# A table in DRAM of the token in each expert slot, biases gathered per slot, a reordered opening, and seven-product multiplications in the first pass

## The chip, the cores and the metric

The kernel runs on one core of one Trainium2 chip. Its time is the device time of one execution in microseconds; of several runs the median is given. The core's engines are TensorE (PE, with its weight loads as PEld), VectorE (DVE), ScalarE (ACT), GpSimd (POOL) and SyncE (SP), which here issues most of the plain DMAs. Everything is computed in fp32.

## The reference

Two layers work on 2048 tokens of width 512 (8 sequences of 256). In the first layer all of this is computed from the normalized tokens:

```python
xn = layernorm(x)
# attention of 32 heads of 128, with decay over the distance of two tokens
q, k, v = silu(xn @ qkv_w.T)            # 3 * 32 * 128 columns
attn = decayed_linear_attention(q, k, v)
attn = rms_normalized(attn) * norm_w
x1 = x + (sigmoid(xn @ gate_w.T) * attn) @ out_w.T
# mixture of experts: 16 experts of inner width 128, two for each token
scores = softmax(xn @ router_w + router_b) + router_bias
gate[t, e] = scores[t, e] for the two best experts of the two best groups, else 0
y = sum_e gate[:, e] * ((silu(xn @ ew1[e] + eb1[e]) * (xn @ ew2[e] + eb2[e])) @ ew3[e] + eb3[e])
# a shared expert, of inner width 256, for every token
z = (silu(xn @ sw1 + sb1) * (xn @ sw2 + sb2)) @ sw3 + sb3
x = x1 + y + z
```

The second layer normalizes again and adds a single-head attention of width 128 and a gated sum of 64 low-rank maps of rank 16, of which each token uses the 16 with the highest scores (`Wr`).

## The kernel before

Tokens are worked on in four chunks of 512 (`NCH`; index `i`), each of four row tiles of 128 (`TPC`; index `t`).

**The opening** (`work1` pool, L140 to L525) goes over the chunks. It loads x (L150, L169), normalizes it (`normalize`, L226), turns it (`turn_rows`, L240, PE transposes into `xT`), multiplies it by the shared expert's first weights (`shared_up`, L317), scores the experts (`route`, L265; `first_two` at L250 compares all pairs of values), and in `shared_down` (L329) multiplies by the shared expert's second weights. There the gates, with a column of ones for the shared expert, are turned (L333), copied (L335) and multiplied by the 17 rows of `b3` (L338): this puts the gated biases of all experts and the shared bias into the same bank as the product (L340), and the bank is added to x (L341), which L349 stores in `xr`. `token_sums` (L369) forms sums of token blocks on POOL, `decays` (L357) the attention's decay tables on ACT, stored in `dec`, and `clear` (L410) fills a quarter of `xd` with zeros: `xd` has 512 columns for each of 6016 expert slots (47 tiles of 128, each tile with a single expert). Then the dispatch (L446 to L523) works out on DVE which slot each token has (`slots`), what its gate is (`slot_gates`) and which weight rows each tile needs (`rows_`). The tiles of the dispatch and its inputs lie in part in the opening's pool, whose memory the next pool, `attn`, takes over.

**The first layer's passes** (L1177 on): chunk `i` against eight groups `g` of four heads. One pair `(i, g)` is a unit, multiplying a 512 x 512 token block by 512 x 2048 weights. The multiplication is done by Strassen's scheme on two levels: on the outer one each unit has seven products (`Outer`, in `ORDER`), on the inner one each of these has seven again (`p1` to `p7`, L1037 to L1066), or eight where it is `plain` (L981). One inner product is four matmuls of 128 x 128 x 128 (`product`, L661, recorded as L666, with two instructions for each). Before, all outers of the first pass (`i == 0`) are plain, and those of the later passes are sevenfold. A sevenfold outer's last product, `p3`, is run inside the next outer.

The weights of an outer are prepared in the first pass (`weights`, L605): a 1 MB block is loaded, outer sums are formed on DVE from further blocks (`st`), four inner sums on POOL (L635), and the result is stored in `ws` for the later passes. Three outers, those in `RAW` (p1, p2, p4), need no outer sums. These steps are popped one by one while the outer before it runs (`following.step()`, L991). `prepare(n + 2)` makes the outer after next; weights are held in a ring of three buffers, blocks `st` and the experts' data in two (`staged`).

PE and DVE are ordered by the scheduler; ACT and POOL keep the program's order in this part (`manual_schedule`, L599). Everything that is not an outer product is a piece put in by `later(n, f)`: it runs `n` products from now. For each quarter of a unit (half of the batch rows, two heads) the pieces are Silu and gate on ACT, scores, attention and output projection on PE. In the first pass, two pieces a unit (`row`, L1086) load a row tile of normalized tokens and scatter it twice into `xd` (L1094). From the second pass on two or three experts per unit are worked in (`expert`, L1080): SP loads 128 rows from `xd` (L696), POOL gathers weights (L697), PE turns the rows 8 products later (L706), multiplies 11 later (L716) and 14 later (L728), ACT copies the result, SP stores it in `yd`. At a chunk's end `load_sum` (L933) loads `xr`, and `finish` (L586) adds the attention. `wrapped_up` (L1145) gathers chunk 0's expert rows, adds them with their gates (`settle`) and normalizes the sum.

**The second layer** (L1258 on) does the same four chunks one after another. `Head` (L1302) holds its router (`route`, 64 columns), `qk`, `values` and `softmax`; for chunk 0 they are run one after another (L1396), for the others as fillers between products.

## Time and profile before

| | |
|---|---|
| median of three runs (lowest, highest) | 2854.79 us (2854.20, 2859.41) |
| the profiled execution | 2856.16 us, span 2854.4 us |
| mean granted clock of TensorE | 0.993 |
| busy share of the span | PE 98%, DVE 55%, ACT 33%, POOL 51% |
| moved by DMA | 763.21 MB, mean 267 GB/s |

The profile is of one execution. An engine's busy time is that of its instructions; issuing DMAs and waiting for semaphores does not count. Matmuls overlap in the pipeline, so the mean duration of one (276 ns for L666) is longer than the step from one to the next, and a PE that is called busy can still run at a low clock; the granted clock is 1.0 at full speed. "x" before a number is a count of instructions, of which an fp32 matmul has two. Where a line shows a number in brackets with an arrow, the engine stood idle so long before, and what follows the arrow is what it waited for. L97 is the helper through which all elementwise tensor operations go, so these are told apart by their tiles.

### The profile page before, as it was taken

How to read it: one execution, taken by the hardware profiler on the slowest of the kernel's cores; microseconds unless marked ns; L12 is line 12 of the kernel's file. 1: busy time of each engine (PE TensorE's matmuls, PEld its weight loads, DVE VectorE, ACT ScalarE, POOL GpSimd, SP SyncE). 2: the span in 40 equal slices, each digit the busy share in tenths (PEclk: the TensorE clock that was granted, in tenths of full speed). 3: DMA queues.
4: the chain of work that ended last, by engine and by line, in shares of the span. 5: the costliest groups of instructions: out<-in, count | busy, mean ns of one | idle time of the engine just before them, and what ended most of it. 6: DMA issues, size and time to landing. Idle time of an engine off the chain costs nothing. (4 is left out here: it accounts for less than half of the span.)

```text
span 2854.4 us, 49572 instructions
## 1 busy us (share of the span) xinstructions
PE 2796.7 (98%) x19864; PEld 2566.1 (90%) x19864; DVE 1569.7 (55%) x2615; ACT 948.2 (33%) x1683; POOL 1465.7 (51%) x1213
## 2 busy tenths in 40 slices
PE   8989999999999999999999999999999999999999
PEld 4469999999999999999999999999999999987877
DVE  6555666666654445444545555555555555556663
ACT  3312222212244333333443333443444333432221
POOL 4545666665546555555645454545544566552210
PEclk9999999999999999999999999999999999999999
DMA  7888998899986777778877777777777788652211
GB/s 255 301 309 337 357 352 341 341 349 347 364 320 246 262 266 273 282 270 299 296 265 257 264 266 265 259 274 280 284 259 259 267 310 298 222 212 88 76 61 61
DMA packets 161943, 763.21 MB, mean 267 GB/s; under 512 B 18209, under 2 KB 24225, under 8 KB 109874
## 3 DMA queue, kind: packets, MB, share of 16 engines
q1 hardware_dynamic: 149826, 706.25, 66.9%
q0 software_dynamic: 11888, 53.79, 5.2%
q8 instruction: 157, 2.57, 0.4%
q14 instruction: 72, 0.59, 0.1%
HBM read 596.14 MB, written 163.05 MB: 266 GB/s over the span
## 5 line engine op out<-in xcount | busy, mean ns | idle before, releaser
L666 PE MATMUL ps_a<-xt,w 128*128 128x128 f32 x5376 | 750.9, 276 | 11.7 <-DVE r L97 7.7
L666 PEld LDWEIGHTS ps_a<-xt,w 128*128 128x128 f32 x5376 | 681.9, 192 | 30.1 <-issue 14.3
L97 POOL TENSOR_TENSOR c<-c 128x512 f32<-128x512 f32 x216 | 271.7, 1273 | 262.0 <-DVE c L97 259.9
L97 POOL TENSOR_TENSOR c<-c,r 128x512 f32<-128x512 f32 x240 | 318.4, 1347 | 158.9 <-DVE r L97 153.1
L666 PE MATMUL ps_e<-xt,w 128*128 128x128 f32 x2688 | 373.4, 275 | 1.3 <-DVE c L97 1.3
L97 POOL TENSOR_TENSOR sums<-sums,sq 128x512 f32<-128x512 f32 x120 | 153.3, 1278 | 426.4 <-ACT sq L796 425.6
L996 ACT COPY cp<-ps_a 128x512 f32<-128x512 f32 x336 | 196.4, 585 | 476.0 <-PE ps_a L666 468.8
L666 PEld LDWEIGHTS ps_e<-xt,w 128*128 128x128 f32 x2688 | 344.4, 192 | 11.2 <-issue 3.8
L97 POOL TENSOR_TENSOR w<-w 128x512 f32<-128x512 f32 x224 | 294.6, 1325 | 108.2 <-issue 31.2
L666 PE MATMUL ps_a<-w,xt 128*128 128x128 f32 x1792 | 346.7, 275 | 0.0
L858 PE MATMUL ps_sc<-wo,gT 128*128 128x256 f32 x1288 | 305.1, 379 | 1.8 <-POOL gT L97 1.8
L97 DVE TENSOR_TENSOR acc<-ps_sc,acc 128x512 f32<-128x512 f32 x208 | 143.3, 690 | 265.8 <-PE ps_sc L858 198.8
L666 PEld LDWEIGHTS ps_a<-w,xt 128*128 128x128 f32 x1792 | 272.3, 192 | 0.0
L97 DVE TENSOR_TENSOR c<-ps_a,c 128x512 f32<-128x512 f32 x232 | 157.9, 686 | 202.7 <-PE ps_a L666 201.7
L858 PEld LDWEIGHTS ps_sc<-wo,gT 128*128 128x128 f32 x1288 | 232.3, 190 | 26.8 <-POOL gT L97 2.0
L666 PE MATMUL ps_b<-xt,w 128*128 128x128 f32 x1680 | 236.4, 277 | 6.8 <-ACT c L1010 4.2
L801 DVE SCALAR_TENSOR_TENSOR gT<-ps_o,nw,c 128x256 f32<-128x256 f32 x256 | 112.0, 479 | 231.0 <-ACT sq L796 222.0
L666 PEld LDWEIGHTS ps_b<-xt,w 128*128 128x128 f32 x1680 | 217.3, 194 | 17.5 <-issue 8.2
L744 ACT ACTIVATE c<-c 128x512 f32<-128x512 f32 x256 | 148.9, 627 | 170.1 <-DVE c L97 170.0
L796 ACT ACTIVATE sq<-ps_o 128x512 f32<-128x512 f32 x120 | 71.6, 597 | 382.3 <-PE ps_o L782 382.3
L666 PE MATMUL ps_e<-w,xt 128*128 128x128 f32 x896 | 173.2, 275 | 0.0
L97 DVE TENSOR_TENSOR s<-ps_sc,decay 128x384 f32<-128x384 f32 x256 | 139.8, 552 | 40.7 <-PE ps_sc L770 38.1
(299 smaller groups left out, 4635.8 us busy)
## 6 DMA issues: line engine op xcount, KB each, us to landing
w<-in_w_att_dram SPq DMA_DIRECT2D x128, 1024.0 KB
st<-in_w_att_dram SPq DMA_DIRECT2D x32, 1024.0 KB
wo<-in_w_out_dram SPq DMA_DIRECT2D x113, 256.0 KB
decay<-dec SPq DMA_DIRECT2D x64, 384.0 KB
w<-ws0p SPq DMA_DIRECT2D x12, 1792.0 KB
w<-ws1p SPq DMA_DIRECT2D x12, 1792.0 KB
w<-ws2p SPq DMA_DIRECT2D x12, 1792.0 KB
w<-ws3p SPq DMA_DIRECT2D x12, 1792.0 KB
```

The source lines that it names most:

```text
L97: (eng or nc.vector).tensor_tensor(o, a, b, op)
L666: mm(bank[:, bass.ts(ty, P)], a, b, start=(first and ty == 0), stop=True, skip_group_check=True,)
L744: nc.scalar.activation(qk, qk, AF.Silu)
L796: nc.scalar.activation(sq, po, AF.Square)
L801: nc.vector.scalar_tensor_tensor(gT[:, h, :].rearrange("p (t n) -> p t n", t=2), po[:, bass.ts(h, S)].rearrange("p (t n) -> p t n", t=2), ...
L858: mm(py[:, bass.ts(t, S)], self.O[p][:, hh, bass.ts(t, P)], self.wo[p][:, hh, :], start=(t == 0 and hh == 0), stop=(hh == 1), skip_group_c ...
L996: nc.scalar.copy(c, bank)
```

## The change

`xd`, its clears and the row loads go. In their place is `table`: 16 equal int32 values, 64 bytes, for each slot, filled with zero at first; `scatter` writes the tokens' numbers into it, five times in a unit of the first pass, and `read_table` reads it in the pass's last unit and turns it into `whose`, one token number for each slot. An expert gathers its rows from the normalized tokens `xnd` by `whose`, later gathers its output bias into the same place by `own_`, and DVE adds it to the product. The shared bias is added on POOL by `last_bias` when `xr` is loaded.

In the opening, chunk 0 is normalized row tile by row tile, two loads of x and that of `wsh` are issued by ACT, sixteen transposes of the identity run on PE first, the router's matmuls stand between the projections (for the last two chunks also in the scheduled order; for the first two, twelve of the sixteen run ahead of the projections), the next chunk is turned before `shared_down` of the last, the two best experts are found with MAX8 and MATCH_REPLACE8, and what the dispatch reads lies in the `acc` tile.

In the first pass p1, p2 and p4 are sevenfold. Their token sums are formed on POOL once (`first_sums`), their weight sums before the outer begins. All outers of the later passes are sevenfold as before; p6, p5, p3 and p7 of the first pass stay plain. The normalization in `wrapped_up` is cut into pieces, and chunk 0's head in the second layer alternates router and q, k projections.

```diff
+    disp = Parts(accp.tile([P, 7 * CH], FP, tag="acc", name="disp"))
...
-        nc.sync.dma_start(out=xs[0][:, t, :], in_=x_t[0, t])
+        (nc.scalar if t % 2 else nc.sync).dma_start(out=xs[0][:, t, :], in_=x_t[0, t])
...
-    nc.sync.dma_start(out=wsh, in_=w_sh)
...
-    b3_t = held[0 : E + 1, SH * C : (SH + 1) * C]
-    nc.sync.dma_start(out=b3_t, in_=b3)
...
-    xd = dram.tile([NSLOT, C], FP, name="xd")
...
+    table = dram.tile([NSLOT, SAME], I32, name="table")
+    none = once([P, NMT * SAME], "none", I32)
+    nc.vector.memset(none, 0)
+    nc.sync.dma_start(out=table.rearrange("(p j) o -> p (j o)", p=P), in_=none)
...
+    root = small.tile([P, TPC], FP, tag="rstd", name="root")
+    nc.scalar.activation(root[:, 0:1], eps_t, AF.Sqrt)
+    nc.scalar.dma_start(out=wsh, in_=w_sh)
...
+    idle = ps_o()
+    for n in range(WARM):
+        nc.tensor.transpose(idle[:, bass.ts(n % 4, P)], ident, ident)
...
+            n.stats(t, tc.keep_in_program_order if behind and t == 0 else lambda ins: ins)
+            if apart:
+                n.root(t, t + 1)
+                n.scaled(t)
+        if not apart:
+            n.root()
+            for t in range(TPC):
+                n.scaled(t)
...
+    def chosen_two(keep, v):
+        top = scratch[:, 0, 0 : TPC * 8].rearrange("p (t n) -> p t n", t=TPC)
+        rest = scratch[:, 0, TPC * 8 : TPC * (8 + E)].rearrange("p (t n) -> p t n", t=TPC)
+        for t in range(TPC):
+            nc.vector.max(top[:, t, :], v[:, t, :])
+        nc.vector.tensor_copy(pair[:, :, 0:2], top[:, :, 0:2])
+        for t in range(TPC):
+            nc.vector.match_replace(rest[:, t, :], pair[:, t, :], v[:, t, :], -NEVER)
+        nc.vector.tensor_scalar(keep, rest, -NEVER, None, ALU.is_equal)
...
+    def scores(pl, xT, t):
+        for c in range(NC):
+            mm(
+                pl[:, bass.ts(t, E)], xT[:, c, bass.ts(t, P)], rw[:, c, :],
+                start=(c == 0), stop=(c == NC - 1),
+            )
...
-        first_two(sel, masked, E)
-        tt(ge[:, :, 0:E], sc, sel, ALU.mult)
-        nc.vector.memset(ge[:, :, E : E + 1], 1.0)
+        chosen_two(sel, masked)
+        tt(ge, sc, sel, ALU.mult)
...
-    def shared_up(i):
+    def shared_up(i, between):
         hT = scratch[:, 2 + i % 2, :].rearrange("p (e n) -> p e n", e=SH)
         for e in range(SH):
             p1, p2 = ps_mm(), ps_mm()
             project(p1, wsh, e, i)
+            between()
             project(p2, wsh, SH + e, i)
+            between()
             h1 = work.tile([P, CH], FP, tag="h1", name="h1")
             b1, b2 = bsh_t[:, 0, e : e + 1], bsh_t[:, 1, e : e + 1]
...
     def shared_down(i, hT):
         xc = xs[i]
-        pg = ps_sc()
-        for t in range(TPC):
-            nc.tensor.transpose(pg[0 : E + 1, bass.ts(t, P)], gates[i][:, t, :], ident)
-        gT = work.tile([E + 1, CH], FP, tag="geT", name="geT", bufs=1)
-        nc.scalar.copy(gT, pg[0 : E + 1, :])
         for t in range(TPC):
             py = ps_mm()
-            mm(py, gT[:, bass.ts(t, P)], b3_t, start=True, stop=False)
             for e in range(SH):
-                mm(py, hT[:, e, bass.ts(t, P)], w3sh[:, e, :], start=False, stop=(e == SH - 1))
+                mm(py, hT[:, e, bass.ts(t, P)], w3sh[:, e, :], start=(e == 0), stop=(e == SH - 1))
             tt(xc[:, t, :], py, xc[:, t, :], ALU.add)
...
+    sel_all = disp.tile([P, NTT, E], FP, name="sel_all")
...
-    for i in range(NCH):
+    def turn(i):
         xT.append(work.tile([P, NC, CH], FP, tag="xT", name=f"xT{i}", bufs=3))
         for t in range(TPC):
             turn_rows(xT[i], xns[i], t, ps_mm())
-        nc.sync.dma_start(out=xnd[i], in_=xns[i])
+    turn(0)
+    for i in range(NCH):
+        nc.sync.dma_start(
+            out=xnd[i * CH : (i + 1) * CH, :].rearrange("(t p) c -> p t c", p=P), in_=xns[i]
+        )
         if i + 1 < NCH:
             begin(i + 1)
         token_sums(i)
@@ -433,12 +473,14 @@
                 w = big("w")
                 nc.sync.dma_start(out=w[:, 0:4], in_=w_att[0, RAW[p]])
                 first_w.append(w)
-        ups.append(shared_up(i))
-        ge = once([P, TPC, E + 1], f"ge{i}")
-        route(xT[i], ge, sel_all[:, bass.ts(i, TPC), :])
+        pl, tiles = ps_sc(), list(range(TPC))
+        ups.append(shared_up(i, lambda: scores(pl, xT[i], tiles.pop(0))))
+        ge = disp.tile([P, TPC, E], FP, name=f"ge{i}")
+        route(pl, ge, sel_all[:, bass.ts(i, TPC), :])
         gates.append(ge)
+        if i + 1 < NCH:
+            turn(i + 1)
         decays(i)
-        clear(i)
         if i > 0:
             share(i - 1, ups[i - 1])
     share(NCH - 1, ups[-1])
...
+    def last_bias(r, t3):
+        nc.sync.dma_start(out=t3, in_=b3[E : E + 1].to_broadcast([P, C]))
+        for t in range(TPC):
+            add(r[:, t, :], r[:, t, :], t3, nc.gpsimd)
...
+                    if o == 6:
...
                 steps += [
-                    partial(inner_sum, *at) for at in ((add, 4, 0, 3), (sub, 5, 4, 1), (sub, 6, 2, 5), (sub, 7, 1, 0))
+                    partial(inner_sum, *at) for at in ((sub, 7, 1, 0), (add, 4, 0, 3), (sub, 5, 4, 1), (sub, 6, 2, 5))
                 ]
+                if p in RAW:
+                    return sums_of(w)
...
         def tokens(i, p):
+            if i == 0 and p in RAW:
+                x_ = first_x[p]
+                return dict(zip(("p1", "p7", "p2", "p3", "p5", "p6", "p4"), (x_[:, n] for n in range(7))))
...
+        for t in first_sums:
+            sub(t[:, 4], t[:, 1], t[:, 0], nc.gpsimd)
+            sub(t[:, 1], t[:, 3], t[:, 1], nc.gpsimd)
+            sub(t[:, 5], t[:, 3], t[:, 4], nc.gpsimd)
+            sub(t[:, 6], t[:, 2], t[:, 5], nc.gpsimd)
...
-                nc.sync.dma_start(out=self.xe, in_=xd[bass.ts(j, P), :])
+                nc.gpsimd.indirect_dma_start(
+                    out=self.xe, out_offset=None, in_=xnd[:, :],
+                    in_offset=bass.IndirectOffsetOnAxis(ap=whose[:, j : j + 1], axis=0),
+                    bounds_check=NT - 1, oob_is_err=False,
+                )
...
+            def bias(self):
+                nc.gpsimd.indirect_dma_start(
+                    out=self.xe, out_offset=None, in_=b3[:, :],
+                    in_offset=bass.IndirectOffsetOnAxis(ap=own_[:, self.j : self.j + 1], axis=0),
+                    bounds_check=E, oob_is_err=False,
+                )
...
-                nc.scalar.copy(ye, py)
+                add(ye, py, self.xe)
...
+                    last_bias(self.r, attn.tile([P, C], FP, tag="sum", name="sb3", bufs=3))
...
                 slot()
+                if self.following:
+                    self.following.step()
...
         def expert(j):
             e = Expert(j)
-            later(8, e.turn)
-            later(11, e.up)
-            later(14, e.down)
-        def row(t):
-            x_ = attn.tile([P, C], FP, tag="sum", name="row", bufs=3)
-            nc.sync.dma_start(out=x_, in_=xnd[t // TPC][:, t % TPC, :])
-            for n in range(TOP):
-                later(6 + 10 * n, partial(scatter, x_, t, n))
-        def scatter(x_, t, n):
+            later(10, e.turn)
+            later(12, e.bias)
+            later(13, e.up)
+            later(18, e.down)
+        def scatter(t, n):
+            token = small.tile([P, SAME], I32, tag="token", name="token")
+            nc.gpsimd.iota(token, pattern=[[0, SAME]], base=t * P, channel_multiplier=1)
             nc.gpsimd.indirect_dma_start(
-                out=xd[:, :],
+                out=table[:, :],
                 out_offset=bass.IndirectOffsetOnAxis(ap=slots[:, n, t : t + 1], axis=0),
-                in_=x_, in_offset=None, bounds_check=NSLOT - 1, oob_is_err=False,
+                in_=token, in_offset=None, bounds_check=NSLOT - 1, oob_is_err=False,
             )
+        def read_table():
+            rows = staged("rows")[0:NMT, 0 : P * SAME]
+            nc.sync.dma_start(out=rows, in_=table.rearrange("(j p) o -> j (p o)", p=P).bitcast(FP))
+            byno = attn.tile([P, P], FP, tag="he", name="byno")
+            def turn_table():
+                nc.vector.tensor_copy(
+                    byno[0:NMT], rows.bitcast(I32).rearrange("j (p o) -> j p o", o=SAME)[:, :, 0]
+                )
+                pt = ps_sc()
+                nc.tensor.transpose(pt[:, 0:NMT], byno[0:NMT, :], ident[0:NMT, 0:NMT])
+                nc.vector.tensor_copy(whose, pt[:, 0:NMT])
+            later(16, turn_table)
...
+            for t in range(TPC):
+                later(35 + 2 * t, partial(stats, t))
+                later(45 + 2 * t, partial(scaled, t))
+            later(43, whole.root)
...
+        def sevenfold(n):
+            return plan[n][0] > 0 or plan[n][2] in RAW
...
                 if i == 0:
-                    for e in range(2):
-                        later(1 + 24 * e, partial(row, 2 * g + e))
+                    for e in range(5 * g, min(5 * g + 5, TOP * NTT)):
+                        later(5 + 10 * (e - 5 * g), partial(scatter, e // TOP, e % TOP))
+                    if g == NG - 1:
+                        later(4, read_table)
...
-            if i == 0:
+            last = outers[n - 1] if n and sevenfold(n - 1) else None
+            if not sevenfold(n):
+                if last:
+                    last.p3()
                 prepare(n + 2)
                 cur.plain(outers[n + 1])
                 continue
+            if i == 0:
+                while cur.steps:
+                    cur.step()
+                cur.following = outers[n + 1]
             cur.p1()
             cur.p7()
-            if plan[n - 1][0] > 0:
-                outers[n - 1].p3()
+            if last:
+                last.p3()
             prepare(n + 2)
             cur.p6()
             cur.p4()
...
             nc.sync.dma_start(out=x_, in_=xr[i])
+            last_bias(x_, work.tile([P, C], FP, tag="sb3", name="sb3", bufs=1))
...
+        def opening(self):
+            self.pf = ps_sc()
+            self.q = work.tile([P, CH], FP, tag="q", name="q1", bufs=1)
+            self.k = work.tile([P, CH], FP, tag="k", name="k1", bufs=1)
+            for n, o in enumerate((self.q, self.k)):
+                pm = ps_sc()
                 for c in range(NC):
-                    mm(
-                        pf[:, bass.ts(t, K)], self.yT[:, c, bass.ts(t, P)], fr_t[:, c, :],
-                        start=(c == 0), stop=(c == NC - 1),
-                    )
+                    mm(pm, wqkv_t[:, c, bass.ts(n, P)], self.yT[:, c, :], start=(c == 0), stop=(c == NC - 1))
+                    if c % 2:
+                        self.ranks(2 * n + c // 2)
+                nc.scalar.activation(o, pm, AF.Identity, bias=bqk_t[:, n : n + 1])
+            self.choose()
...
     head = Head(0)
-    head.route()
-    head.qk()
+    head.opening()
```

## The prediction

> **What bounds the kernel now.** I read the page first, then a table of stretches, PE's waits and the timeline of the places that the table pointed to. The table gives us, then busy us and instructions of PE, PEld, DVE, ACT, POOL, then PE's granted clock, DMA share and GB/s.
>
> ```profile
> PE 2796.7 (98%) x19864; PEld 2566.1 (90%) x19864; DVE 1569.7 (55%) x2615; ACT 948.2 (33%) x1683; POOL 1465.7 (51%) x1213
> ...
> 40.00:50.00 10.00, 10.00 (x29) 6.11 (x29) 9.55 (x14) 2.58 (x5) 10.00 (x14) 0.68 0.15 59
> ...
> 140.00:160.00 20.00, 16.25 (x33) 5.34 (x32) 10.06 (x15) 0.57 (x1) 12.21 (x18) 0.83 0.88 328
> ...
> 164.00:176.00 12.00, 7.80 (x68) 7.37 (x67) 10.56 (x32) 0.67 (x2) 0.00 (x0) 1.00 0.51 176
> 176.00:200.00 24.00, 19.99 (x150) 19.30 (x151) 13.45 (x23) 6.18 (x10) 7.24 (x6) 0.93 1.00 376
> 240.00:773.00 533.00, 530.10 (x4107) 511.51 (x4106) 331.76 (x508) 119.34 (x206) 319.87 (x250) 1.00 0.91 346
> ```
>
> PE is the bound nearly everywhere, so time is gained only by giving it less work or by closing its gaps. Two stretches are soft. In the opening (to 164 us) PE is called busy, but at a clock of 0.68 or 0.83 in places, and a busy matmul there is not at its pace. Between 164 and 200 PE stands still for about 8 us. The first pass (164 to about 763, where the first expert's gather issues) is full.
>
> The timeline shows the opening's last chunk (start us, us, engine, line, op, count, and the idle time before it with its releaser):
>
> ```profile
> 130.65 0.60 PE L333 MATMUL ps_sc<-ident,ge 128*17 128x128 f32 x4
> 131.28 0.57 ACT L335 COPY geT<-ps_sc 17x512 f32<-17x512 f32 x1 [4.88 <-PE ps_sc L333]
> 131.91 1.12 PE L338 MATMUL ps_b<-held,geT 17*128 17x512 f32 x2 [0.67 <-ACT geT L335]
> 132.96 1.98 PE L340 MATMUL ps_b<-held,scratch 128*128 128x512 f32 x4
> 134.87 1.12 PE L338 MATMUL ps_a<-held,geT 17*128 17x512 f32 x2
> ...
> 147.41 0.61 PE L333 MATMUL ps_sc<-ident,ge 128*17 128x128 f32 x4 [3.58 <-DVE ge L97]
> ...
> 175.97 1.55 PE L666 MATMUL ps_b<-xt,w 128*128 128x128 f32 x6 [4.20 <-ACT c L1010]
> ```
>
> The steps between starts are the prices: the expert bias costs 1.26 us for turning the gates and 1.05 us per row block, and the shared expert itself 1.91 us per block. At 147 PE waits for the router's chain; at 176 for ACT's first copies, which wait for the opening's memory.
>
> [...]four projection matmuls of 512 columns (x8 in the trace) take 5.34 us just after the narrow router matmuls and 3.44 us later. [...] Here POOL is held 1.01 us by one gather (L697); its landing the trace doesn't show.
>
> **The change, part by part.** The sum stands against the profiled execution: 2856.16 us, span 2854.4, so 1.8 us around it; the median of three is 2854.79, which is 1.4 lower.
>
> *Opening.* At full pace a chunk costs PE: 16 transposes 1.75 (four of 0.44), router 1.7, projections four of 3.44 = 13.7, shared-down four of 1.91 = 7.6: 24.8 us, four chunks 99.2. Before, from the first transpose (10.2) to the first attention product (164.4) it is 154.2 us. The bias matmuls and gate transposes, four times 1.26 + 4 x 1.05 = 5.46, are 21.8 and vanish. The other 33 us are waits and half clock: 3.6 us at the end for the router's chain and half clock after it (5.7 us for a block of 2.96), 5.2 us for the first router group instead of 1.7, 5.3 to 5.6 us for the first projection of each chunk. Of these go: the loss at the end, since the changed instruction order has no gate transposes and puts two shared-downs (15.3 us) between the last router matmul and the dispatch; most cold groups, since the last two chunks spread the router between projections[...]. The router's choice sheds five DVE steps on 1024 elements (two of 1.44, 1.59, 1.44, 1.21 us) for four MAX8 and four MATCH_REPLACE8 (0.22 and 0.21 us by layer 2's rows, plus 0.08 for each value load): about 5 us less per chunk. The first transpose moves from 10.2 to about 7.5, as each block is scaled when its own statistics are done and the Sqrt table (1.28) is loaded ahead. So 7.5 + 99.2 + 1 for the dispatch = 108 with nothing lost, 135 with all other losses kept. I take 120, as chunks 0 and 1 still run twelve router matmuls in a block and ACT still waits for decay stores. **Gain 44.** Cover needed: POOL's token sums, about 20 us a chunk (4 of 1.3 to 1.6, 28 of 0.45 to 0.55) against 25 us of PE; twelve extra (5.4 us) run before chunk 1 arrives. The four clears of xd (12.3 MB) leave SP's queue, of 45 MB moved up to 160 us; the table's fill is 0.4 MB. Two loads of x and the one of wsh move to ACT's queue, where nothing ran before 7.7 us; wsh is first read at about 12, and before it was there at 18.6 from an issue at 4.1, so its landing is one of the things that the 12 us of loss cover.
>
> *After the opening.* ACT's copies no longer wait for DVE's dispatch, but for the last store of x (1 MB, 3 to 7 us), and now the third product already needs a copy, where eight ran free before. Before lost 12.8 us of PE waits from 176 to 773 (4.2, 2.2, 1.7 and small ones). I take 4 for the copy and the rest as it was: nothing gained.
>
> *First pass.* p1, p2 and p4 go from eight products to seven: 3 x 8 units x 4 matmuls = 96 (the instruction orders say 6496 and 6400). A four-matmul product steps 0.89 us in the timeline (476.54 to 477.43), 0.2225 a matmul: **21.4 us less**, on the path since PE is full. POOL: per unit of 74.8 us (598.5 over 8) it now has 28 weight sums x 1.324 + 4 x 1.277 + 4 scatters x 1.08 = 46.5 us, 62%. Six result sums of 1.3 come in, five scatters with an iota replace four: 56 us of about 72, 78%. The weight sums of the three now gate PE, one outer ahead. Also the loads of the outer two ahead are issued three products later, behind the deferred p3, on SP. DVE already waits on such loads (11.8 + 9.6 us in this pass). Cost between 0 and 21; I take 3, for POOL keeps slack in the plain outers and banks hold some six products of lead.
>
> *Experts.* Per expert, SP's load of rows (256 KB, 47) becomes a gather, a second gather brings the bias, DVE adds (0.69) where ACT copied (0.58). DVE is at half load there. POOL gets 94 x 1.01 = 95 us, over 1500 us in which it is at 53%. Behind a gather wait POOL's sums for results, behind those ACT's Silu and copies, behind these PE. The turn now has ten slots of some 1.3 us from the gather[...]. Bounds 0 and 10 us; I take 3. The scatters fall from 256 KB each to 128 rows of 64 bytes, and 16 row loads of 256 KB go. The table's read in unit 7 takes one load on SP, one of the two stage buffers for 16 slots, one PE transpose and two DVE copies; the weight block that would want that buffer is p7's, loaded later than the copy frees it, so I count nothing (0 to 3).
>
> *Last bias.* Three times four POOL sums (5.1 us) wait for a load in SP's queue in mid-stream, and four more in layer 2 under low_rank. Bounds 0 and 12; I take 3.
>
> *Layer 2.* The first normalization is cut into pieces: before, PE waited 2.6 us for DVE's mv and 1.7 for r there; I take 4 less. The head's router is put between the q and k projections:
>
> ```profile
> 2553.32 5.36 PE L1316 MATMUL ps_sc<-wsm 128*128 128x64 f32 x32
> 2558.47 8.86 PE L1310 MATMUL ps_sc<-wsm 128*128 128x512 f32 x16
> ```
>
> The next chunks' same groups take 3.52 and 6.87, so up to 3.8 to be had; I take 3.5.
>
> Sum: -44 - 21.4 + 3 + 3 + 3 - 4 - 3.5 = -64 on 2856.2, so 2792.
>
> **Rivals.** *The opening is paced by transfers.* 33 MB stay in the opening; at the mean of before (45 MB in 160 us, 283 GB/s) they need 118 us and the copies then wait for the landings, so the first pass starts at 135: 2807. For it: DMA share 1.0 at 10 to 40 us. Against: 59 GB/s at 40 to 50, so the queue often stood idle. *POOL becomes the bound of the first pass* and the sevens bring nothing: 2810. For it: 78%, in order, with waits for DVE and ACT in between. Against: the later passes hold PE at 99% with POOL at 53% and every sum gating. *Slower:* an expert's rows are late. POOL issues the gathers behind sums that wait for DVE, PE stands at the turn, 47 times. It decides from 64/47 = 1.4 us per expert; at 3 us it ends at 2930. Against: the weights' gather, three times larger, was never seen to hold PE at the eleventh slot. *It doesn't do what it says* is excluded for the matmul counts by the instruction order; for the warm clock it is in the range.
>
> **The numbers.** Likeliest case 0.62 (2792, own range 2774 to 2806), transfers 0.18, POOL 0.15, late rows 0.03, the rest 0.02 on either side. So 2792 us, range 2772 to 2822. Faster 0.95, same (within 0.2%, 5.7 us, what a measurement can tell) 0.015, slower 0.035.
>
> **What would show it.** Right: first attention product near 120; no row of K 17; no wait of 3 us for the router; the first expert's gather near 763 - 62 = 701; POOL near 75% in between; PE at 99% from there on. Wrong: PE waits for POOL's w or for DVE's c in the first pass beyond 10 us together (POOL rival); a clock under 0.9 and ACT waiting for dec stores in the opening (transfers); waits of PE for xw or xeT (slower).

## The result, and the profile after

The changed kernel takes 2823.71 us (median of four, 2820.53 to 2825.62) where the kernel before took 2857.10 in the same runs: the ratio is 0.9881, 95% interval 0.9863 to 0.9898. It is faster by 33.4 us, about half of the 64 that were predicted, and lies just beyond the stated range (2772 to 2822). Its profiled execution took 2825.62 us, with a span of 2823.9, and PE's mean granted clock is 0.993 as before. From here on line numbers are those of the changed kernel; in the experiments some are off by one to four.

The engines' busy time, then the stretches that answer to those shown of before (us, then busy us and instructions of PE, PEld, DVE, ACT, POOL, PE's granted clock, DMA share, GB/s):

```profile
PE 2753.2 (97%) x19641; PEld 2541.2 (90%) x19641; DVE 1626.7 (58%) x2722; ACT 950.7 (34%) x1685; POOL 1642.1 (58%) x1414
```

```profile
40.00:50.00 10.00, 10.00 (x24) 4.38 (x23) 9.62 (x28) 7.16 (x10) 9.92 (x16) 0.99 0.57 216
100.00:119.70 19.70, 19.70 (x61) 10.05 (x61) 12.71 (x46) 2.20 (x3) 8.91 (x15) 1.00 0.68 259
119.70:131.70 12.00, 10.15 (x91) 9.96 (x90) 11.49 (x32) 3.56 (x7) 1.19 (x1) 1.00 0.92 336
131.70:155.70 24.00, 20.95 (x172) 19.98 (x171) 19.88 (x34) 5.05 (x8) 16.88 (x14) 1.00 0.83 315
195.00:713.00 518.00, 497.90 (x3795) 477.42 (x3794) 355.63 (x520) 134.60 (x234) 372.00 (x315) 0.99 0.86 322
```

PE lost 43.5 us of busy time, but its share fell from 98% to 97%: new gaps opened. The opening's end is at full clock now, and the first pass, which missed 3 us of 533 before, misses 20 of 518. The timeline of PE shows the opening's end: the last two of eight blocks of the shared expert, which run from 104.91 us without a break, a little dispatch (L525 to L527), and the first attention product.

```profile
115.29 1.88 PE L379 MATMUL ps_e<-held,scratch 128*128 128x512 f32 x4
117.01 1.88 PE L379 MATMUL ps_a<-held,scratch 128*128 128x512 f32 x4
118.72 0.59 PE L525 MATMUL ps_sc<-disp 128*128 128x256 f32 x2
119.16 0.59 PE L526 MATMUL ps_sc<-disp 128*128 128x256 f32 x2
119.59 0.29 PE L527 MATMUL ps_sc<-disp 128*128 128x16 f32 x2
119.73 0.91 PE L724 MATMUL ps_a<-xt,w 128*128 128x128 f32 x6
```

Four points of the program, in both traces, tell where the gain goes:

| point | before | after | gain |
|---|---|---|---|
| first attention product | 164.38 | 119.73 | 44.7 |
| first copy of the pass with experts | 764.32 | 712.90 | 51.4 |
| last sum of squares of layer 1 | 2553.2 | 2517.0 | 36.2 |
| end of the span | 2854.4 | 2823.9 | 30.5 |

So 15 us are lost in the passes with experts and 6 in layer 2, and the first pass gained 6.8 where 18.4 were predicted. Two executions can differ by some us in such a stretch: the trace of e12 below, whose opening and layer 2 are those of the kernel before, took 2.5 us more than it to the first point and 4.2 less in layer 2. So the 6 us of layer 2 are not clear of that. A finer ruler is DVE's 128 gate products (L801 before, L878 after), four in each unit. By it the gain grows from 42 to 65.5 us at the third product of the first pass's seventh unit, drops by 15.7 at the next, falls by 11 more over chunk 1 (from 49.0 to 38.4), by 3.8 at that chunk's end, and rises by 5.3 over the last three units.

The drop of 15.7 is one stall, in the timeline of all engines:

```profile
645.31 0.30 SPq L1181 DMA_DIRECT2D rows<-table  x1
666.43 0.26 DVE L1185 CAST byno<-rows 47x128 f32<-47x128 int32 x1 [13.34 <-DMA rows<-table]
667.38 1.15 ACT L821 ACTIVATE c<-c 128x512 f32<-128x512 f32 x2 [10.81 <-DVE c L100]
668.33 3.61 PE L955 MATMUL ps_sc<-wo,gT 128*128 128x256 f32 x8 [8.82 <-DVE gT L878]
673.49 2.83 POOL L100 TENSOR_TENSOR w<-w 128x512 f32<-128x512 f32 x2 [13.40 <-DVE w L100]
```

DVE stands 13.3 us at the cast of the table, which lands 21 us after its issue; ACT, POOL and PE stand for DVE. In the passes with experts (715 to 2215 us) PE waits among others for these (us in total, times, longest):

```profile
PE ps_sc L793 <- DVE xeT L777: 7.7, 6, 1.3
PE ps_a L724 <- DVE r L100: 6.3, 14, 1.1
PE ps_e L724 <- DVE c L100: 6.1, 2, 4.4
PE ps_sc L1024 <- DVE ye L100: 2.1, 1, 2.1
```

### The profile page after: what moved, and what is told of

It reads as the page before. It is cut to its first block, busy times and chain, and to the rows that moved or that the text cites. A ratio compares the mean times of both kernels' runs of the same rounds, so it can differ in the third digit from the quotient of the medians.

```text
span 2823.9 us, 49588 instructions
## 1 busy us (share of the span) xinstructions
PE 2753.2 (97%) x19641; PEld 2541.2 (90%) x19641; DVE 1626.7 (58%) x2722; ACT 950.7 (34%) x1685; POOL 1642.1 (58%) x1414
## 4 chain that ended last, share of the span: by engine, by line
PE 80%; DVE 7%; DMA 5%; issue 4%; POOL 3%; ACT 0%; SPq 0%; DVEq 0%; POOLq 0%; ACTq 0%
PE ps_a L724 23%; PE ps_e L724 12%; PE ps_sc L935 9%; PE ps_b L724 6%; PE ps_o L858 3%; PE ps_sc L846 3%; PE ps_sc L955 3%; PE ps_sc L793 3%; PE ps_o L859 2%; PE ps_a L1651 2%; PE ps_sc L847 2%; DVE w L100 1%; PE ps_a L1573 1%; PE ps_sc L805 1%; DVE r L100 1%
## 5 line engine op out<-in xcount | busy, mean ns | idle before, releaser
L724 PE MATMUL ps_a<-xt,w 128*128 128x128 f32 x5376 | 751.0, 276 | 13.3 <-DVE r L100 7.1
L100 POOL TENSOR_TENSOR c<-c 128x512 f32<-128x512 f32 x240 | 302.7, 1276 | 251.1 <-DVE c L100 242.7
L100 POOL TENSOR_TENSOR c<-c,r 128x512 f32<-128x512 f32 x264 | 347.0, 1335 | 173.1 <-DVE r L100 171.6
L1077 ACT COPY cp<-ps_a 128x512 f32<-128x512 f32 x384 | 224.1, 584 | 607.7 <-PE ps_a L724 586.5
L100 DVE TENSOR_TENSOR c<-ps_a,c 128x512 f32<-128x512 f32 x216 | 146.9, 688 | 140.7 <-PE ps_a L724 135.6
L878 DVE SCALAR_TENSOR_TENSOR gT<-ps_o,nw,c 128x256 f32<-128x256 f32 x256 | 112.0, 479 | 190.5 <-ACT sq L873 182.2
L724 PE MATMUL ps_b<-xt,w 128*128 128x128 f32 x1536 | 214.1, 276 | 7.0 <-issue 5.5
L724 PEld LDWEIGHTS ps_b<-xt,w 128*128 128x128 f32 x1536 | 195.0, 192 | 14.8 <-issue 11.0
```

The lines of the kernel that those rows point to most:

```text
L100: (eng or nc.vector).tensor_tensor(o, a, b, op)
L724: mm(bank[:, bass.ts(ty, P)], a, b, start=(first and ty == 0), stop=True, skip_group_check=True,)
L878: nc.vector.scalar_tensor_tensor(gT[:, h, :].rearrange("p (t n) -> p t n", t=2), po[:, bass.ts(h, S)].rearrange("p (t n) -> p t n", t=2), ...
L1077: nc.scalar.copy(c, bank)
```

## The experiments

All are compared by their ratio to the kernel before, run beside them (changed kernel: 0.9881; 0.001 is 2.9 us). Many start from the first, with its 48 tiles; the medians of different sets differ by some us (the kernel before took 2853.4 to 2862.3 in them). The interval of a ratio is some 5 us to either side, so smaller differences between two experiments rest on their traces.

### The table's read

**e1_table48**

```diff
+NR = 48
-    table = dram.tile([NSLOT, SAME], I32, name="table")
+    table = dram.tile([NR * P, SAME], I32, name="table")
...
-            rows = staged("rows")[0:NMT, 0 : P * SAME]
+            rows = staged("rows")[0:NR, 0 : P * SAME]
```

> The changed kernel with a table of 48 slot tiles in place of 47, so that the read in unit 7 has 48 outer rows. Theory: in the changed kernel that read (385 KB from 47 outer rows) lands some 20 us after its issue and PE loses about 12 us behind it; with 48 rows it lands in under 5 us, the loss goes, and the time is 2811 us (2808 to 2815) where the changed kernel has 2823.7. Rival: the loss in unit 7 comes from DVE's and POOL's queues (two more DVE copies ahead of the sums) and not from the landing: within 3 us of 2823.7. Both expect everything outside 640 to 690 us unchanged.

2812.13 us, ratio 0.9835 (0.9818 to 0.9853): 12 to 13 us less by one more tile. From its timeline:

```profile
643.75 0.34 SPq L1182 DMA_DIRECT2D rows<-table  x1
649.77 0.33 SPq L668 DMA_DIRECT2D st<-in_w_att_dram  x1
651.46 0.94 DVE L1186 CAST byno<-rows 48x128 f32<-48x128 int32 x1
659.96 0.68 DVE L101 TENSOR_TENSOR w<-w,st 128x512 f32<-128x512 f32 x1
```

The cast starts 7.7 us after the issue, without a wait. By the trace's semaphore updates the read landed 4.6 us after it. The weight block issued 6 us behind it (`st`, L668) landed 4.8 us after its own issue, and the sum that reads it, at 659.96, doesn't wait either. What makes a read of 48 rows land after 4.6 us where that of 47 took 21.1 (changed kernel) was not shown.

**e14_cover** moved the turn of the table away from the read: `later(16, turn_table)` became `later(36, turn_table)`, with 47 tiles.

> The changed kernel with its table of 47 tiles, but with the turn of the table 36 slots after the read instead of 16. Nothing left out. Theory: the read is slow (some 20 us), and only its lateness costs; with 36 slots of cover PE loses nothing: 2812 (2809 to 2815), as with 48 tiles. Rival: the slow read also holds up other transfers of SP's queue or the staging buffer, so part of the loss stays: 2817 or more.

2821.52, ratio 0.9881 (0.9862 to 0.9901): nothing. But it had not moved what stalls. DVE's order is the scheduler's, and DVE's cast stood between the same two sums as before, waiting 11.9 us; only PE's transpose had moved. **e16_cover** held the cast back too:

```diff
-                nc.vector.tensor_copy(
+                tc.keep_in_program_order(nc.vector.tensor_copy(
...
-            later(16, turn_table)
+            later(36, turn_table)
```

> As the run before with the table of 47 tiles and the turn 36 slots behind the read, but with DVE's cast of the read rows held in program order: in the run before, DVE's order had the cast at the same place as in the changed kernel (between the same two sums), so that only PE's transpose had moved. Nothing left out. Theory, only lateness costs: no wait of DVE for the table, 2812 (2809 to 2815). Rival, the slow read holds up other transfers or the staging buffer for the next loads: 2817 or more.

2821.92, ratio 0.9865 (0.9848 to 0.9881). The wait for the table is gone, and DVE stands 7.8 us at a weight block instead, where the changed kernel waited 1.6. From the timelines of SP's queue, DVE and PE, and then two lines of the changed kernel:

```profile
642.95 0.30 SPq L1181 DMA_DIRECT2D rows<-table  x1
648.97 0.33 SPq L667 DMA_DIRECT2D st<-in_w_att_dram  x1
668.42 2.50 DVE L100 TENSOR_TENSOR w<-w,st 128x512 f32<-128x512 f32 x4 [7.76 <-DMA st<-in_w_att_dram]
696.60 0.25 DVE L1185 CAST byno<-rows 47x128 f32<-47x128 int32 x1
```

```profile
670.42 1.62 PE L724 MATMUL ps_b<-xt,w 128*128 128x128 f32 x6 [4.66 <-DVE w L100]
```

```profile
651.33 0.33 SPq L667 DMA_DIRECT2D st<-in_w_att_dram  x1
671.46 2.50 DVE L100 TENSOR_TENSOR w<-w,st 128x512 f32<-128x512 f32 x4 [1.59 <-DMA st<-in_w_att_dram]
```

A weight block of 1 MB (`st`), issued 6 us behind the read, lands 19.4 us after its issue. The changed kernel has the same delay, hidden in part by the wait for the table: there the block issued at 651.33 lands after 20.0 us, and the sums at 671.46 wait for it. In both traces fifteen of the block's sixteen semaphore updates come within 6 us and the last one some 14 us after these. With 48 rows (e1 above) the same block took 4.8 us. So the rival holds: the read delays transfers that come behind it. By the gate products the stall is 8.0 us shorter, and 6.6 are given back at the next one. The read could not be hidden in this way; it had to be made fast.

### The experts' slots

An expert's pieces stood at 8 (turn), 11 (up) and 14 (down) products after its start; the change put them at 10, 13 and 18, with the bias gather at 12. **e2_down22** (`later(18, e.down)` to `later(22, e.down)`) tested my first reading, that DVE's add of the bias waits for its gather:

> The changed kernel with the last step of an expert (the down product and the add of its bias) at slot 22 in place of 18; nothing is left out. Theory: DVE stands at the add of the bias for a gather that lands late (1.76 us in a unit of chunk 1), its later copies are late by that, and PE loses 1.3 us in each of seven units at the turned rows: with four more slots of cover 9 us go, 2815 (2812 to 2818). Rival: the loss of chunk 1 comes from DVE having the add at all, or from the third gather on POOL: no more than 3 us to 2823.7.

2826.7, ratio 0.9885 (0.9866 to 0.9903): no gain. PE's wait for xeT was gone, and in its place came 17.6 us for r and 5.0 for an expert's rows. **e5_no_bias** took the bias out:

```diff
-            later(12, e.bias)
...
-                add(ye, py, self.xe)
+                nc.scalar.copy(ye, py)
```

> With the table of 48 tiles (2812 us), and without the experts' bias: no third gather on POOL, and ACT copies the expert's result as in the kernel before. Left out: the experts' third bias. It prices the whole edit. Theory: the third gather and DVE's add together cost the 10 us that the experts of chunk 1 lost (units of three experts): 2801 (2798 to 2804). Rival: the rows' gather on POOL, where before SP loaded them, is what costs it: within 3 us of 2812.

2812.32, ratio 0.9841 (0.9819 to 0.9863): the bias as a whole costs nothing measurable, and PE's wait for xeT was still there (9.5 us, seven times). My theory fell. **e6_act_copy** kept the gather and made only the second of these edits:

> With the table of 48 tiles (2812 us): the third gather is issued as before, but its rows are not used, ACT copies the expert's result instead of DVE's add. Left out: the experts' third bias in the sum. Theory A, DVE's add in DVE's full stretch is the cost: 2801, as without the bias at all. Theory B, the gather on POOL is the cost: no more than 3 us below 2812.

2817.77, ratio 0.9857 (0.9832 to 0.9882): no gain either. By the medians it is about 6 us slower than with 48 tiles alone, though the intervals overlap, and in the trace PE's waits for r rose from 7.1 to 12.4 us; taking the add off DVE doesn't pay. What was left was the place. **e12_old_slots** is the kernel before with three numbers changed:

```diff
-            later(8, e.turn)
-            later(11, e.up)
-            later(14, e.down)
+            later(10, e.turn)
+            later(13, e.up)
+            later(18, e.down)
```

> The kernel before, with nothing of the change but the slots of an expert: turn 10, up 13, down 18 instead of 8, 11, 14. Theory (the place alone costs it): PE waits about 1.3 us in each of seven units and the time is 2857 plus 9, 2866 (2862 to 2869). Rival (the gathers or the bias cost it): 2857, within 3 us.

2863.03, ratio 1.0023 (1.0013 to 1.0033), 6.6 us slower than the kernel before, or 4.5 by the medians; chunk 1 alone, from its first product to that of chunk 2, takes 614.2 us instead of 606.9. PE's wait is the one of the changed kernel to the digit:

```profile
PE ps_sc L716 <- DVE xeT L708: 7.7, 6, 1.3
```

DVE's timeline shows why, in the changed kernel and then in the kernel before:

```profile
936.82 0.68 DVE L100 TENSOR_TENSOR r<-ps_a,cp 128x512 f32<-128x512 f32 x1
937.41 3.47 DVE L100 TENSOR_TENSOR c<-c,r 128x512 f32<-128x512 f32 x2
940.81 0.68 DVE L777 COPY xeT<-ps_sc 128x512 f32<-128x512 f32 x1
```

```profile
979.89 1.79 DVE L97 TENSOR_TENSOR c<-c,r 128x512 f32<-128x512 f32 x1
981.61 0.68 DVE L97 TENSOR_TENSOR r<-ps_b,cp 128x512 f32<-128x512 f32 x1
982.21 0.67 DVE L708 COPY xeT<-ps_sc 128x512 f32<-128x512 f32 x1
```

Two products later the copy stands behind two sums `c<-c,r` instead of one. Such a sum has both inputs in SBUF and took 1.73 us in the changed kernel's lines and 1.79 in those of before, beside POOL's sums, where a sum with one input in PSUM took 0.68. In the changed kernel's whole trace, the 52 sums `c<-c,r` with POOL's sums beside them all along took 0.96 to 1.80 us (median 1.75; in the kernel before 54 of them, 0.84 to 1.80, median 1.38), 79 sums of two SBUF inputs (`w<-w,st`) with no POOL sum beside them took 0.68 to 0.69 us, and a sum with one input in PSUM took 0.69 also where POOL worked all along. The trace of e12 has the same two slow sums (1.79 and 1.75 us) ahead of the copy. By what mechanism POOL's sums lengthen these was not shown.

Why then were the slots moved? **e9_turn8** put turn, bias and up at 8, 10 and 11:

> With the table of 48 tiles (2812 us): an expert's turn, bias gather and up products at slots 8, 10 and 11 (the kernel before has turn and up at 8 and 11), down still at 18. Nothing left out. Theory: PE's wait of 1.29 us for the turned rows, once in each unit of chunk 1 and there with and without the bias, comes from the place: two products later the turn's DVE copy falls behind DVE sums that run beside POOL's and take nearly twice as long. At 8 and 11 the wait goes: 2802 (2800 to 2805). Rival: the rows' gather lands too late or POOL's third DMA issue is the cost, wherever the turn stands: 2812 or more, with PE waiting for xw.

2830.49, ratio 0.9893 (0.9875 to 0.9912): 17 to 18 us slower than with 10, 12 and 13. The wait for xeT is gone but for 1.8 us; now the gathered rows are late, as the rival had it:

```profile
PE ps_sc L776 <- DMA xw<-xnd,whose: 18.9, 9, 2.9
```

In that trace the 47 gathers of rows land 3.7 to 8.8 us after their issue (median 6.5), a time for which the prediction had no trace; the nine turns that wait come 7.3 to 8.9 us after theirs. With the turn at ten it comes at least 10.1 us after (e1). What was expected of this run was missed: eight slots cost more than the place behind the two sums.

**e10_up14** left the turn at 10 and moved up from 13 to 14:

> With the table of 48 tiles (2812 us): up at slot 14 instead of 13, turn still at 10: one product more between the transposes and their first reader. Nothing left out. Theory: DVE's copy of the turned rows is 1.3 us late and a product is 0.9 us, so most of the wait goes: 2804 (2801 to 2807). Rival: DVE and POOL have no slack in these units, and PE waits for the next reader (r of p7 or p4) instead, as it did when the down product was moved: 2812.

2804.01, ratio 0.9812 (0.9797 to 0.9828), 7 to 8 us less than with 48 tiles alone, and no wait for xeT in the trace (8.6 us in e1's). The two intervals overlap; the trace decides: chunk 1 takes 608.8 us against 619.3 in e1 and 606.9 in the kernel before.

### The shared expert's bias at the chunk ends

At the end of chunk 0 POOL waits, in order, for the load of x, and then works 5 us on the four sums; the next expert's bias gather and what waits for it stand behind:

```profile
736.28 4.96 POOL L100 TENSOR_TENSOR spare<-spare,sb 128x512 f32<-128x512 f32 x4 [10.41 <-DMA spare<-xr]
```

**e3_last_spread** put the sums later:

```diff
-            add(r[:, t, :], r[:, t, :], t3, nc.gpsimd)
+            put(8 + t, partial(bias, t))
```

> The changed kernel with the four POOL sums of the shared expert's bias put 8 to 11 slots after the load of x that they read, instead of right behind its issue, with the bias row in a buffer of the output weights' ring. Theory: POOL stands about 10 us for that load at each of three chunk ends and what is queued behind it (gathers, sums of results) makes PE lose about 1.4, 4.4 and 1.7 us there: 2817 (2814 to 2820). Rival: PE's loss at the chunk ends is the sum of POOL's work there, four sums of 1.27 us, wherever they stand: within 2 us of 2823.7.

2826.56, ratio 0.9881 (0.9862 to 0.9900): nothing in all. By the gate products chunk 0's end gains 3.3 us, chunk 1's nothing, and chunk 2's loses 4.5. Chunks 1 and 2 end with seven POOL sums that combine the products; that the late bias sums come on top of these is likely, and not shown. **e7_no_last** left the bias of the shared expert out:

> With the table of 48 tiles (2812 us), and without the shared expert's bias: no load of its row and none of the four POOL sums at the four chunks. Left out: that bias. It prices the edit. Theory: PE's waits at three chunk ends (2.1, 4.4 and 1.7 us) and 1.9 us of the wait for cp at chunk 3 of layer 2 go: 2803 (2800 to 2806). Rival, from the run with the sums spread: the chunk ends are bound by POOL's other work and nothing but the wait in layer 2 goes: 2810.

2798.99, ratio 0.9794 (0.9772 to 0.9817), 12 to 13 us less. By the gate products 3.9 of them are at the end of chunk 0 and 3.5 at chunk 1's; in layer 2 PE's wait for cp falls from 3.6 us (e1) to 0.4. Chunk 2's end gains nothing. **e11_open** added the same bias elsewhere, by DVE in the opening:

```diff
+        for t in range(TPC):
+            add(xs[i][:, t, :], xs[i][:, t, :], sb3)
```

> With the table of 48 tiles (2812 us): the shared expert's bias added in the opening, by 16 DVE sums of 0.69 us on x after it was normalized, instead of by POOL at the chunk ends; nothing left out. Theory: without these POOL sums the kernel takes 2799, and DVE is 55% busy in the opening, so 2801 (2798 to 2804). Rival: the 11 us of DVE sums delay the router or the copies of turned blocks in the opening, up to 8 us: 2808.

2811.45, ratio 0.9839 (0.9822 to 0.9857): no gain over e1, and beyond the rival's 2808 too. The first gate product comes 11.0 us later, as long as sixteen sums of 0.69 us: DVE's busy share says nothing of slack in the opening. What the chunk ends gave was paid there, by about as much. **e15_mix** spread the sums of chunk 0 alone, with 48 tiles and up at 14:

> Nothing left out: table of 48 tiles, up at slot 14, and chunk 0's four sums of the shared expert's bias 8 to 11 slots behind their load (the other chunks as in the changed kernel). Theory: 2804 less the 3.3 us that the spread gave at the end of chunk 0: 2801 (2798 to 2804). Rival: with the other waits gone the end of chunk 0 is bound by POOL anyway: 2804.

2802.74, ratio 0.9815 (0.9798 to 0.9833): 3.0 us less at that chunk's end, but not to be told from e10 in the time.

### The head, the normalization, the opening and the sevens

**e4_head** (`head.route()` and `head.qk()` in place of `head.opening()`):

> The changed kernel with layer 2's first head in the old order: router, choice, then the q and k projections, instead of the router's matmuls between the projections. Theory: the tail of the changed kernel is 5.7 us longer than before because the choice comes later and DVE's chain holds the values and the first low rank products; the old order gives back 3 to 6 us, 2819 (2817 to 2821). Rival (the step of the prediction): the old order costs 3.5 us[...]: 2827.

2823.23, ratio 0.9870 (0.9849 to 0.9891): theory and rival both missed, for the order makes no difference in the time. The first three lines are the old order (e4), the next three the changed kernel:

```profile
2516.86 5.79 PE L1433 MATMUL ps_sc<-wsm 128*128 128x64 f32 x32
2522.45 8.41 PE L1429 MATMUL ps_sc<-wsm 128*128 128x512 f32 x16
2536.69 0.60 PE L1530 MATMUL ps_sc<-ident,G 128*64 128x128 f32 x4
```

```profile
2526.70 1.00 PE L1433 MATMUL ps_sc<-wsm 128*128 128x64 f32 x8
2527.53 3.79 PE L1496 MATMUL ps_sc<-wsm 128*128 128x128 f32 x32
2535.26 0.83 PE L1530 MATMUL ps_sc<-ident,G 128*64 128x128 f32 x3 [2.21 <-DVE v L100]
```

From the head's start to the values takes 10.5 us (2517.07 to 2527.53) instead of 13.8, 3.4 less, as the step said. But the choice starts later, PE waits 2.2 us for DVE behind it, and by 2543.9 both have reached the same product (2543.86 in the changed kernel, 2543.90 in e4).

**e18_norm** put the first normalization of layer 2 in one piece again, on e10:

> With the table of 48 tiles and up at slot 14 (2804 us), and the first normalization of layer 2 in one piece again, right behind its last sum, as in the kernel before. Nothing left out. The step of the prediction: PE waits 2.6 us for mv and 1.7 us for r again, 2808. The milestones of the two kernels differ by 5.3 us over the last two units, so up to 2809.5. Rival: that difference is a shift of work between units, and the time stays within 1.5 us of 2804.

2810.18, ratio 0.9826 (0.9810 to 0.9842): 4 to 6 us slower, with PE's waits of 2.6 for mv and 1.7 for r back. The intervals of the two overlap, but the waits that came back, 4.3 us together, agree with the 4 that the prediction had for the pieces.

**e17_router** put the router's matmuls into one block:

> With the table of 48 tiles (2812 us), and the router's sixteen matmuls of every chunk in one block ahead of the projections. Nothing left out. The step of the prediction: [...]both late chunks get 1.7 us longer and the first attention product comes 3.4 us later, 123; 2815. Rival: the router's choice starts earlier and the dispatch with it, which gives as much back: first product at 120 or before, 2812.

2823.43, ratio 0.9864 (0.9848 to 0.9881), 8 to 11 us slower than with 48 tiles alone, more than theory and rival had it. The first product comes at 129.3, not 123. From PE's timeline of it:

```profile
33.49 5.40 PE L312 MATMUL ps_sc<-rw,xT 128*128 128x16 f32 x32 [0.26 <-DVE xT L282]
38.73 5.36 PE L356 MATMUL ps_b<-xT,wsh 128*128 128x512 f32 x8
58.74 0.74 PE L277 MATMUL ps_a<-ident,xn 128*128 128x128 f32 x4 [3.04 <-DVE scratch L372]
```

The theory's 1.7 us for a late chunk are the difference of the changed kernel's first projections, 5.3 us in chunk 1 and 3.6 in chunks 2 and 3. In this run the one behind chunk 2's block takes 3.68 us and the one behind chunk 3's 6.47, so a block alone does not make it slow. The block itself runs slowly in chunk 1 (5.4 us; 3.64 in chunk 2, 4.23 in chunk 3), and DVE's work on the router comes before the operation (L372) that frees the bank which PE then waits for. Against one block of all 32 instructions the spread order is worth 9.0 us of the opening (129.3 against 120.3 in e1). That is no share of the 44.7, for the kernel before ran only part of these matmuls in a block.

**e8_plain** undid the sevens of the first pass (`sevenfold` without `or plan[n][2] in RAW`):

> With the table of 48 tiles (2812 us), and with the outers p1, p2 and p4 of the first pass in eight products again (96 matmuls of four columns blocks more), nothing left out. Theory: the sevens bring nearly their 21.4 us, as POOL keeps slack: 2832 (2829 to 2835). Rival: POOL's sums and later loads cost part of it and the sevens bring no more than 12: 2824 or less.

2827.84, ratio 0.9896 (0.9871 to 0.9921): against e1 the sevens are worth 15.7 us by the medians, 17 by the ratios, 11.3 by the spans of the profiled executions. In the first pass itself, from its first attention product to that of chunk 1, they save 15.9 us (596.4 to 580.5). By its median the run lies below what was expected and above the rival's bound.

### The sum

**e13_sum** joins e1, e10 and e7, so it too leaves the last bias out:

> Table of 48 tiles, up at slot 14, and no bias of the shared expert (left out: that bias). If the three terms that the prediction had too small (the table's read, the experts' slots, the last bias) are separate, their gains add up: 2812 less 8 less 13, 2791 (2788 to 2794). Rival: they share waits of POOL and DVE in the same units, and part of the gain is counted twice: 2797 or more.

2791.11, ratio 0.9770 (0.9753 to 0.9788). The three gains add up.

## Why the prediction was wrong

The sign was right, and no rival took over, but four terms of the sum were mis-sized, all in the same direction.

| term | predicted, us | measured, us | by |
|---|---|---|---|
| opening | -44 | -44.7 | first attention product |
| sevens, with what they cost | -18.4 | -15.9 in the pass, -11 to -17 in all | e8 |
| normalization in pieces | -4 | -4 to -6 | e18 |
| table's read | 0 (0 to 3) | +12 to 13 | e1 |
| experts' slots | +3 (0 to 10) | +5 to 8, in chunk 1 alone 7 to 10.5 | e10, e12 |
| last bias | +3 (0 to 12) | +12 to 13 | e7 |
| head's order | -3.5 | 0 | e4 |

The last four are off by about 12, 4, 10 and 3.5, some 30 us together; the miss is 31.7. The sevens missed by 2.5 in the pass itself, and the stalls just after the opening, taken as unchanged, fell by 3.3, from 8.2 to 4.9 us (the two stretches of 36 us). These two misses cancel: with 48 tiles the whole first pass takes 580.5 us where it took 598.8, 18.3 less, beside 18.4 predicted, which is partly luck. With the first three of the four mended the chip gives 2791.1. That run leaves out the bias, for which the prediction had 3 us, so its counterpart is 2789, not 2792; both are closer than the single terms are known.

*Opening.* Right to the microsecond in its end, 119.7 for 120, and no wait of 3 us for the router is left. But this is partly luck, for the terms inside are off. From PE's timeline of the changed kernel:

```profile
80.81 1.88 PE L379 MATMUL ps_b<-held,scratch 128*128 128x512 f32 x4
82.53 1.88 PE L379 MATMUL ps_a<-held,scratch 128*128 128x512 f32 x4
87.68 3.60 PE L355 MATMUL ps_b<-xT,wsh 128*128 128x512 f32 x8
91.12 0.96 PE L311 MATMUL ps_sc<-rw,xT 128*128 128x16 f32 x8
91.93 3.68 PE L355 MATMUL ps_a<-xT,wsh 128*128 128x512 f32 x8
```

The router steps 0.81 us for one row tile, so 3.2 for a chunk; the 1.7 of the prediction is what sixteen of a chunk's 32 instructions take. The shared expert steps 1.72 a block, not 1.91. A chunk at full pace (79.03 to 104.91) takes 25.9 us, not 24.8, and the losses left are some 7 us (an estimate from the slow groups), not 12. They lie in chunks 0 and 1: there 24 router instructions run in one block, and the projection behind takes 5.5 and 5.3 us instead of 3.6, at a clock of 0.68 in chunk 1 (37 to 42 us). The clock is 0.50 there from 36.9 to 40.1 us, and in chunk 0 from 9.5 to 19.5; in the kernel before, where the prediction speaks of half clock, it is 0.50 from 40 to 44 and from 150 to 153. Ahead of these two in chunk 1 PE had been busy without a break since 8.23 us, so no idle stretch comes before the drop there; what lowers the clock was not shown. Behind eight router instructions no projection was slow (3.68 us at 91.93), and from 42 to 105 us the clock is 1.00. The sixteen transposes of the identity that run first did not spare chunk 0 its slow groups (5.14 and 5.49 us, before 5.14 and 5.60). And in e17, where the clock is 0.93 from 60 to 129 us (changed kernel 1.00 from 60 to 119.7), it is not the clock alone that costs, because DVE's order goes with the router's.

*First pass.* The rival that POOL becomes the bound is not what happened: POOL's busy share was 72% (372.0 of 518 us), predicted 75 to 78, and the largest of PE's gaps, 8.8 of the 20.1 us in which it stood idle from 195 to 713, was DVE at the table. With 48 tiles gaps of 9.1 us remain, 3.2 of them for POOL's w, where the kernel before had 2.9 us from 240 to 773. The sign that the prediction had named for this rival, waits for POOL's w and DVE's c beyond 10 us together, came to 5.6.

*Table.* The failing step is "loaded later than the copy frees it, so I count nothing". I looked at who would want the buffer, not at how long the read takes. 385 KB were treated like any load, but with its 47 outer rows this one landed after 21.1 us, where a 1 MB weight block, with 128, landed after 4.8 (e1). The step was false in its own words too: in the changed kernel p7's block is issued at 666.72, right behind the cast that frees its buffer (666.43), and with 48 rows at 657.82, well after that cast (651.46).

*Experts.* I priced the gathers on POOL and the landing time that ten slots leave, and took 3. The bias with its gather costs nothing that e5 shows; the gather of the rows stayed in every run, so its own cost is not known. What costs is that two reading pieces moved by two products, into a place where DVE is full: I had named the new slots and never looked at what DVE does there. The rival of late rows was real, at eight slots (e9) and not at ten.

*Last bias.* The mechanism and the upper bound (12) were right, the value taken was not. POOL in order behind a load, at the point where a chunk's end already waits for POOL, should have been taken near its bound. My own sum has 5.1 us of POOL work four times; e7 shows more than half of it on PE's path.

*Head.* PE's part came as computed. What was late next, DVE's choice behind the last router matmul, was not in the sum.

Open is a part of layer 2's loss: between the first two chunks PE waits 2.2 us for DVE's normalized rows, where it waited 1.5 in two pieces before. In e12, whose layer 2 is the one of the kernel before, such a wait is 1.96 us, so it may be no loss. No run was made for it.

The best version with nothing left out, 48 tiles and up at 14, takes 2804.0 us (e15, with chunk 0's sums spread, 2802.7), against 2823.7 and 2857.1.

## What to carry to other kernels

Before counting a small load at nothing, look at its outer dimension: 47 rows and 48 differed by 12 us here (landings of 21.1 and 4.6). A piece that is moved must be priced at its new place on every engine that it touches, above all on one that runs in order and slows down beside another (DVE's sums `c<-c,r`, 0.68 us alone and up to 1.80 beside POOL's). And where a term has bounds of 0 and 12, ask whether the waiting engine is one that the end of a stage already needs; if so, lean to the upper end, which was right here.

## What the runs showed of the hardware

A 385 KB read from DRAM with 47 outer rows landed after 20 to 21 us (21.1 in the changed kernel, 19.7 in e14, 20.4 in e16), and with 48 rows after 4.6 us (e1). A 1 MB load issued 6 us behind it on the same queue landed after 20.0 us (changed kernel) and 19.4 (e16), against 4.8 behind the read of 48 rows. A gather of 128 rows of 2 KB by POOL landed after 3.7 to 8.8 us (e9). DVE's sum of two SBUF operands (128 x 512 fp32) took 0.68 to 0.69 us alone and, as `c<-c,r` with POOL's sums beside it all along, 0.96 to 1.80 (median 1.75); with one operand in PSUM it took 0.68 to 0.69 also beside them. In the kernel before, a table load on ACT took 1.28 us (mean of each group of them), and the opening's last store of x (1 MB) landed after 4.8.
